# Copies, relus and banks of the last group moved between VectorE and ScalarE, and two orders in the second step, in a fused four-layer graph network

## The chip, the cores and the metric

The kernel runs on one core of a Trainium2 chip. The time is the device time of one execution in microseconds (us); lower is better. It is stated as the median of several executions. The profile is of one further execution.

## The reference, cut to what matters

The input is 128 graphs of 64 nodes with 512 features, float32, and one 64x64 adjacency matrix for each graph. Four layers follow each other, and each is a residual with a layer norm behind it: `x = layernorm(x + layer(x, adj))`.

```python
# layer 0: two hypergraph convolutions, widths 512 -> 1024 -> 512
h = layer_norm(relu(hypergraph_conv(x, adj, W1, b1)), gamma, beta)
y = hypergraph_conv(h, adj, W2, b2) + x
# layer 1: attention by scores of the nodes
s = (x @ w) @ a
A = s[..., :, None] + s[..., None, :]
A = jnp.tanh(A / 8.0) * 8.0
A = jnp.where(A >= 0, A, 0.1 * A)          # the leaky step
A = jnp.exp(A) * A_shape                   # then rows normed, scaled; A @ x @ w
# layer 2: three graph convolutions
x = relu(adj @ (x @ W1) + b1); x = relu(adj @ (x @ W2) + b2); out = adj @ (x @ W3) + b3
# layer 3: attention with 8 heads of 64
out = (0.33 * softmax(q k^T / 8) + 0.33 * adj + 0.33 * exp(-dist)) @ v   # by head
out = out @ W_out + b_out
```

## The kernel before, in words

**Groups.** The 128 graphs are 64 pairs (two graphs fill 128 partitions), and four pairs make a group, so there are 16 groups, numbered 0 to 15. A group's data is one tile of 128 x 4 x 512. `first_half` (for group 0, `first_group`) runs layers 0 and 1 of a group, and `second_half` runs layers 2 and 3. For the last group, number 15, the end of layer 3 is written out on its own in `last_rows`.

**Steps.** Work of three groups is interleaved by a list of names for each step (`start`, `step_1`, `order`, `step_last`, `rest_last`): layers 0 and 1 of group q, layer 2 and the scores of group q-1, and the attention and output of group q-2. The second step, `step_1`, holds layers 0 and 1 of group 1 beside layer 2 of group 0. In most steps a scheduler then orders each engine's instructions by readiness; `behind(key)` forbids it to place an instruction ahead of another one that was noted in `last_add`. `in_turn(engine)` keeps an instruction behind the newest one of that engine. In the start, and for TensorE (PE) and VectorE (DVE) in the last step, everything is in written order.

**Products.** `multiply` makes a 512x512 by 512x512 product with seven block products in place of eight (`B11, T1, T2, B21, T3, B22, T4`, in this order). Each is `product`: 8 recorded matmuls of 128x256, 1.73 us in the trace. `Left.sums` prepares the left side by four VectorE operations `s1` to `s4`: `B11` needs none of them, `T1` needs `s1`, `T2` needs `s2`. In the result, `u1`, `u5`, `u2` are copies of partial sums out of PSUM (the matmul's memory), and four additions or copies write the four quadrants. The block products `B11`, `T2`, `T3` and `T4` add up in one PSUM bank, tile `a`: so `T4` can't start before the addition that reads the bank after `T3` (line 589) is done. The names in the profile are those of the tiles: `a_l2c`, `b_l2c`, `c_l2c` are the banks of layer 2's third product, and so on.

**Small matmuls.** `graph_T` multiplies by the adjacency and turns the result; it fills two PSUM tiles for each half of a group (`duo`), one for each graph of the pairs, which are then copied out. With `both=True` ScalarE (ACT) copies the first of the two and VectorE the second (line 490).

**The end.** `last_rows` turns the last group's softmax (`turn_probs`), multiplies by v (`attend`, tiles `pv`), scales by 0.33 while it copies out (`taken`), and then computes the output pair by pair with `rows_of` (tiles `pp`): addition, statistics (`bn_stats`, `bn_aggr`), square root on ScalarE, reciprocal, scaling, and a store by SyncE (SP). The last pair's two column halves share one PSUM bank, and each half is added and measured on its own.

The queue of a DMA is that of the engine that issues it; all loads and stores in the stretches around the change are on SP. GpSimd (POOL) writes derived weights to DRAM.

Of the kernel before, what the change touches and what calls it, by code (L numbers as in the profile page):

```python
# [8 lines left out]
FP = mybir.dt.float32  # L9
# [5 lines left out]
P = 128  # L15
# [26 lines left out]
def kernel(  # L42
# [427 lines left out]
    def graph_T(src, mat, dst, duo, key, both=False):  # L470

        ps = [ps_gt.tile([P, 4, 2, C], FP, name=f"gt_{key}_{duo}_{g}", tag="gt") for g in range(2)]
        for c in range(4):
            for p in range(2):
                for f in range(2):
                    for g in range(2):
                        rows, c0 = slice(g * C, (g + 1) * C), c * P + f * C  # L480
                        ten.matmul(  # L481
                            ps[g][f * C : (f + 1) * C, c, p, :],
                            src(2 * duo + p)[rows, c0 : c0 + C],
                            mat[rows, 2 * duo + p, :],
                            start=True, stop=True,
                        )
        o = dst[:, :, duo * Q : (duo + 1) * Q].rearrange("p c (a g i) -> p c a g i", a=2, g=2)
        for g in range(2):
            if both and g == 1:
                vec.tensor_copy(o[:, :, :, g, :], ps[g])  # L490
            else:
                act.copy(o[:, :, :, g, :], ps[g])  # L492
# [8 lines left out]
    def behind(key):  # L501
        return tc.issue_after(last_add[key]) if key in last_add else nullcontext()
# [117 lines left out]
    def turned(t):  # L620

        return lambda m, n: t[:, 2 * n : 2 * n + 2, m * Q : (m + 1) * Q]
# [126 lines left out]
    def first_half(g):  # L749
# [83 lines left out]
        yield "w2"  # L833
        with behind(f"l2c_{q - 1}.u2"):
            act.activation(t, t, AF.Tanh, scale=0.125)
        vec.scalar_tensor_tensor(t, t, 0.1, t, ALU.mult, ALU.max)
# [13 lines left out]
        left = Left(f"l1_{q}")  # L850
        for duo in range(2):
            with behind("agg_0.p") if q == 1 else nullcontext():
                graph_T(pair, t, left.t, duo, f"l1_{q}", both=True)
        yield "c3"
        with behind(f"wo_{q - 2}"):
            left.sums()
# [39 lines left out]

    def rows_of(p, ts, quads, u0=0, u1=None, ps=None, ns=range(2)):

        if ps is None:
            ps = ps_acc.tile([P, 2, Q], FP, name=f"pp_{p}", tag="acc")  # L900
        us = range(len(ts))[u0:u1]
        for n in ns:
            for u in us:
                for c in range(KD):
                    ten.matmul(
                        ps[:, n, :], ts[u][:, c, p * P : (p + 1) * P], quads[u][c // 2, n][:, c % 2],
                        start=(n == 0 and u == 0 and c == 0), stop=(u == len(ts) - 1 and c == KD - 1),
                        skip_group_check=True,
                    )
        return ps  # L910
# [162 lines left out]
    def second_half(g):  # L1073
# [18 lines left out]
                    turned(h1.t)(m, n)[:, c], src[:, c], AF.Relu, bias=gb1_col[:, 2 * n + c : 2 * n + c + 1]  # L1092
                )

        for _ in multiply([left], (w_g[0], q), turned(h1.t), f"l2a_{q}", flipped=True, then=relu if q == 0 else None):
            yield "l2a1"
        if q > 0:
            for c in range(KD):
                act.activation(h1.t[:, c, :], h1.t[:, c, :], AF.Relu, bias=gb1_col[:, c : c + 1])
        h1.sums()  # L1100
# [5 lines left out]
        adt = grp.tile([P, G, C], FP, name=f"adt_{q}", tag="adt", bufs=1)  # L1106
        act.activation(adt, g["atc"], AF.Exp, scale=-1.0)
        g["adt"] = adt
        if alone:
            shifted(g, f"l2b_{q}")  # L1110
        yield "gb3"

# [2 lines left out]
        for c2 in range(2):  # L1115
            ps = [ps_gt.tile([P, 2, G, C], FP, name=f"gth2_{q}_{c2}_{h}", tag="gt") for h in range(2)]
            for c in range(2):
                for p in range(G):
                    for f in range(2):
                        for h in range(2):  # L1120
                            rows, c0 = slice(h * C, (h + 1) * C), (2 * c2 + c) * P + f * C
                            ten.matmul(  # L1122
                                ps[h][f * C : (f + 1) * C, c, p, :],
                                g2[rows, p, c0 : c0 + C], g["atc"][rows, p, :], start=True, stop=True,
                            )
            for c in range(2):
                k = 2 * c2 + c
                o = h2.t[:, k, :].rearrange("p (d h t) -> p d h t", d=2, h=2)
                for h in range(2):
                    act.activation(  # L1130
                        o[:, :, h, :], ps[h][:, c].rearrange("p (d a) i -> p d (a i)", d=2),
                        AF.Relu, bias=gb2_col[:, k : k + 1],
                    )
        if not alone:
            shifted(g, f"l0w2_{q + 1}.u2")
        h2.sums()
        yield "gh"
        g3 = big.tile([P, G, D], FP, name=f"g3_{q}", tag="big")
        gen = multiply([h2], (w_g[2], q), nat(g3), f"l2c_{q}", stops=(3, 6),
# [29 lines left out]
        for duo in range(2):  # L1169
            ps = [ps_gt.tile([P, KD, 2, C], FP, name=f"xtp_{q}_{duo}_{h}", tag="gt") for h in range(2)]  # L1170
            for c in range(KD):
                for p in range(2):
                    for h in range(2):
                        rows = slice(h * C, (h + 1) * C)
                        with behind("l1w_1.p6") if q == 0 else nullcontext():
                            ten.transpose(
                                ps[h][:, c, p, :], xg[rows, 2 * duo + p, c * P : (c + 1) * P], identc[rows]
                            )
            o = left.t[:, :, duo * Q : (duo + 1) * Q].rearrange("p c (a g i) -> p c a g i", a=2, g=2)
            for h in range(2):  # L1180
                act.copy(o[:, :, :, h, :], ps[h])  # L1181
        left.sums()
        yield "xT"
        qT = big.tile([P, KD, T], FP, name=f"qT_{q}", tag="big")
# [48 lines left out]
    def last_rows(g, probs, v, left):  # L1233

        q, xg = g["q"], g["x"]
        o = out[q * T : (q + 1) * T, :].rearrange("(p t) d -> t p d", t=P)
        gen = multiply([left], (w_v, q), nat(v), f"v_{q}", stops=(3, 6))
        next(gen)
        yield "v1"
        steps = [[softmax_steps(g, duo, probs[duo], h2) for h2 in range(2)] for duo in range(2)]  # L1240
        for n in range(2):
            for h2 in range(2):
                next(steps[0][h2])
        for n in range(2):
            next(steps[1][0])
        for h2 in range(2):
            next(steps[0][h2])
        next(gen)
        yield "v2"
        left = Left(f"oT_{q}")  # L1250
        pts = turn_probs(g, 0, probs[0])
        whole(gen)
        yield "v"
        taken(0, attend(g, 0, pts, v), left)
        for n in range(2):
            next(steps[1][1])
# [7 lines left out]
        def added(p, ps, n=None):  # L1264
            cols = slice(0, D) if n is None else slice(n * Q, (n + 1) * Q)
            row = xg[:, p, cols]
            vec.tensor_add(row, ps.rearrange("p n f -> p (n f)")[:, cols], row)

        def written(p):
            layer_norm(xg, f"l3_{q}_{p}", (p,))  # L1270
            nc.sync.dma_start(out=o[:, p], in_=xg[:, p])

        ps = projected(0)
# [23 lines left out]
        nc.sync.dma_start(out=o[:, 3], in_=xg[:, 3])  # L1297
        yield "o"

    def softmax_steps(g, duo, ds, h2):  # L1300
# [90 lines left out]
                        )  # L1391
        return ps

    def taken(duo, ps, left):
        o4 = left.t[:, :, duo * Q : (duo + 1) * Q].rearrange("p c (a g i) -> p c a g i", a=2, g=2)
        for gg in range(2):
            act.mul(o4[:, :, :, gg, :], ps[gg], LA)  # L1397

# [177 lines left out]
```

## Time and profile before

| | |
|---|---|
| time, median of 3 runs | 2743.45 us (2742.39 to 2743.74) |
| profiled execution, its own time | 2741.53 us |
| its span, first to last instruction | 2739.8 us |
| TensorE busy | 2720.2 us (99%) |
| VectorE busy | 2079.1 us (76%) |
| ScalarE busy | 804.2 us (29%) |
| DMA | 405.14 MB, mean 148 GB/s |

The profiled execution takes 1.7 us more than its span, and 1.9 us less than the median of the runs. In the views below, the first number of a row of the timeline is its start in us from the start of the span, the second how long it lasted; what stands in brackets is for how long the engine was idle before it, and which instruction of which engine ended that. A row with a count (x8) stands for several instructions merged. A matmul's record overlaps the next one's: they start 0.216 us apart and each lasts 0.379 us.

### The profile page before, as it was taken

To read this page: it belongs to the slowest core of one execution; us is meant where nothing else is said; L and a number is where in the kernel's file an instruction comes from. 1 tells how busy PE (TensorE), PEld (TensorE's weight loads), DVE (VectorE), ACT (ScalarE), POOL (GpSimd) and SP (SyncE) were. 2 spreads that over 40 slices of the span, in tenths; PEclk is the share of its full clock that TensorE was granted. 3 is DMA by queue.
4 is the path that set the end of the run, shared out by engine and by line. 5 is a ranking of instruction groups with operands and counts; after the bars stand their busy time and mean duration, and the time that the engine had idled before them with its cause. 6 is when DMAs were issued, how large, how long until landed. Compare 5 with 4: busy or idle time off the path is not lost.

```text
span 2739.8 us, 67717 instructions
## 1 busy us (share of the span) xinstructions
PE 2720.2 (99%) x28770; PEld 2348.2 (86%) x28770; DVE 2079.1 (76%) x4119; ACT 804.2 (29%) x1442; POOL 38.0 (1%) x71
## 2 busy tenths in 40 slices
PE   9999999999999999999999999999999999999998
PEld 8878888888888888888888888888888888888887
DVE  6877687876877778787786877778777687776866
ACT  3323323232232332322223232232323323232232
POOL 2000000000000000000000000000000000000000
PEclk9999999999999999999999999999999999999999
DMA  8534454454544545445454454545545455454541
GB/s 263 180 120 153 121 174 141 141 166 131 171 132 139 166 129 169 132 143 169 132 166 130 144 164 131 166 126 153 159 131 171 130 161 146 132 164 131 151 126 60
DMA packets 309388, 405.14 MB, mean 148 GB/s; under 512 B 57408, under 2 KB 185184, under 8 KB 309088
## 3 DMA queue, kind: packets, MB, share of 16 engines
q1 hardware_dynamic: 304256, 385.58, 47.4%
q0 software_dynamic: 4832, 15.24, 1.5%
q8 instruction: 228, 3.74, 0.6%
q14 instruction: 72, 0.59, 0.1%
HBM read 369.78 MB, written 30.93 MB: 146 GB/s over the span
## 4 chain that ended last, share of the span: by engine, by line
PE 95%; DVE 3%; ACT 1%; issue 0%; DMA 0%; POOL 0%; DVEq 0%; POOLq 0%
PE a_l0w L539 15%; PE b_l0w L539 7%; PE a_l2b L539 4%; PE a_q L539 4%; PE a_k L539 4%; PE a_l2a L539 4%; PE a_v L539 4%; PE c_l0w L539 4%; PE a_l1w L539 4%; PE a_wo L539 4%; PE a_l2c L539 4%; PE gt_l L481 3%; PE gt_l0h L481 2%; PE b_l1w L539 2%; PE b_l2a L539 2%; PE b_l2b L539 2%
## 5 line engine op out<-in xcount | busy, mean ns | idle before, releaser
L539 PE MATMUL a_l0w<-w2w,aT_l0h 128*128 128x256 f32 x720 | 164.3, 381 | 0.0
L457 DVE BATCH_NORM_STATS2 st_l<-x 128x6 f32<-128x512 f32 x244 | 157.7, 673 | 0.6
L539 PEld LDWEIGHTS a_l0w<-w2w,aT_l0h 128*128 128x128 f32 x720 | 135.6, 190 | 18.8
L463 DVE TENSOR_SCALAR x<-x,mv_l,rs_l 128x512 f32<-128x512 f32 x244 | 119.3, 542 | 2.2
L539 PE MATMUL b_l0w<-w2w,s_l0h 128*128 128x256 f32 x480 | 108.5, 379 | 0.0
L779 ACT ACTIVATE h<-h 128x1024 f32<-128x1024 f32 (+1 forms) x58 | 54.9, 947 | 178.5 <-DVE h L598 157.5
L539 PEld LDWEIGHTS b_l0w<-w2w,s_l0h 128*128 128x128 f32 x480 | 91.1, 190 | 12.5
L1130 ACT ACTIVATE aT_h<-gth,gb_col 128x256 f32<-128x256 f32 x128 | 48.5, 492 | 159.0 <-PE gth L1122 159.0
L447 ACT ACTIVATE rs_l<-mv_l,eps_t 128x4 f32<-128x4 f32 (+1 forms) x64 | 19.0, 297 | 257.0 <-DVE mv_l L458 245.3
L555 DVE TENSOR_TENSOR u_l0w<-a_l0w,b_bc 128x512 f32<-128x512 f32 x56 | 38.6, 690 | 69.2 <-PE a_l0w L539 69.2
L492 ACT COPY aT_l<-gt_l 128x512 f32<-128x512 f32 x146 | 77.1, 596 | 45.7 <-PE gt_l L481 45.7
L539 PE MATMUL a_l1w<-ww,aT_l 128*128 128x256 f32 x360 | 85.7, 381 | 2.1 <-issue 2.1
L539 PE MATMUL a_l2b<-gwbw,aT_h 128*128 128x256 f32 x360 | 86.6, 383 | 0.7 <-ACT aT_oT L1397 0.7
L539 PE MATMUL a_l2c<-gwcw,aT_h 128*128 128x256 f32 x360 | 86.3, 382 | 0.0
L539 PE MATMUL a_q<-aT_xT,wqw 128*128 128x256 f32 x360 | 85.1, 379 | 0.7 <-ACT aT_xT L1181 0.7
L539 PE MATMUL a_l2a<-aT_l,gwaw 128*128 128x256 f32 x360 | 85.0, 379 | 0.0
L539 PE MATMUL a_k<-aT_xT,wkw 128*128 128x256 f32 x360 | 85.0, 379 | 0.0
L539 PE MATMUL a_l0w<-w1aw,aT_l 128*128 128x256 f32 x336 | 80.8, 383 | 0.0
L539 PE MATMUL a_v<-wvw,aT_xT 128*128 128x256 f32 x336 | 80.8, 383 | 0.0
L539 PE MATMUL a_wo<-wow,aT_oT 128*128 128x256 f32 x336 | 79.5, 379 | 0.0
L539 PE MATMUL a_l0w<-w1bw,aT_l 128*128 128x256 f32 x336 | 79.4, 379 | 0.0
L539 PEld LDWEIGHTS a_l1w<-ww,aT_l 128*128 128x128 f32 x360 | 68.5, 190 | 11.6 <-issue 2.3
(528 smaller groups left out, 6488.4 us busy)
## 6 DMA issues: line engine op xcount, KB each, us to landing
w2w<-w2k SPq DMA_DIRECT2D x210, 256.0 KB, 2.6
x<-in_x_dram SPq DMA_DIRECT2D x15, 1024.0 KB, 5.7
w1aw<-w1ak SPq DMA_DIRECT2D x60, 256.0 KB, 2.6
w1bw<-w1bk SPq DMA_DIRECT2D x60, 256.0 KB, 2.7
ww<-wk SPq DMA_DIRECT2D x60, 256.0 KB, 2.8
gwaw<-gwak SPq DMA_DIRECT2D x60, 256.0 KB, 3.1
gwbw<-gwbk SPq DMA_DIRECT2D x60, 256.0 KB, 2.7
gwcw<-gwck SPq DMA_DIRECT2D x60, 256.0 KB, 2.7
```

The lines of the kernel that those rows point to most:

```text
L447: act.activation(rs[:, at], mv[:, at, 1], AF.Sqrt, bias=eps_t)
L457: vec.bn_stats(st, xg[:, p, :])
L463: vec.tensor_scalar(xg[:, p, :], xg[:, p, :], mv[:, p, 0:1], rs[:, p : p + 1], ALU.subtract, ALU.mult)
L481: ten.matmul(ps[g][f * C : (f + 1) * C, c, p, :], src(2 * duo + p)[rows, c0 : c0 + C], mat[rows, 2 * duo + p, :], start=True, stop=True,)
L492: act.copy(o[:, :, :, g, :], ps[g])
L539: ten.matmul(acc[:, blk, :], lhsT, rhs, start=(first and blk == 0 and i == 0), stop=(last and i == n_k - 1), skip_group_check=True,)
L555: last_add[f"{key}.{what}"] = (act.copy(t, ps) if res is None else vec.tensor_add(t, ps, res(m, n))).ins
L779: act.activation(hn, hn, AF.Relu)
L1130: act.activation(o[:, :, h, :], ps[h][:, c].rearrange("p (d a) i -> p d (a i)", d=2), AF.Relu, bias=gb2_col[:, k : k + 1],)
```

## The change

For the last group (15):

- Layer 2's first product applies its relu quadrant by quadrant, as group 0 does, straight behind each addition; the fourth quadrant's relu reads PSUM in place of a copy.
- The relus behind the second product's `gth2` tiles are split: h = 0 on ScalarE, h = 1 on VectorE, as an addition and a maximum. The bias additions and mask work of `shifted` move from ahead of the sums of `h2` to behind them.
- The copies of `xtp` are split in the same way, and so are those of attention's first half (`taken(0, ...)`), whose ScalarE part is now placed ahead of the last exponential.
- In the output of the last pair, each column half has a PSUM bank of its own, so pair 3's matmuls don't wait for an addition. The statistics of pair 2 are interleaved with those of pair 3. The last scaling is made in two halves of 256 columns, each with a store of its own, one issued by SP and one by ScalarE.

In the second step (group 1 beside group 0):

- Both copies of each `gt_l1_1` duo are on ScalarE (`both=q > 1`).
- The leaky operation stands behind the addition after `T3` of `l2c_0` (`l2c_0.d`).

```diff
-        vec.scalar_tensor_tensor(t, t, 0.1, t, ALU.mult, ALU.max)
+        with behind("l2c_0.d") if q == 1 else nullcontext():
+            vec.scalar_tensor_tensor(t, t, 0.1, t, ALU.mult, ALU.max)
...
-                graph_T(pair, t, left.t, duo, f"l1_{q}", both=True)
+                graph_T(pair, t, left.t, duo, f"l1_{q}", both=q > 1)
...
-        if ps is None:
+        fresh = ps is None
+        if fresh:
...
-                        start=(n == 0 and u == 0 and c == 0), stop=(u == len(ts) - 1 and c == KD - 1),
+                        start=(fresh and n == ns[0] and u == 0 and c == 0), stop=(u == len(ts) - 1 and c == KD - 1),
...
-        for _ in multiply([left], (w_g[0], q), turned(h1.t), f"l2a_{q}", flipped=True, then=relu if q == 0 else None):
+        for _ in multiply([left], (w_g[0], q), turned(h1.t), f"l2a_{q}", flipped=True, then=relu if alone else None):
             yield "l2a1"
-        if q > 0:
+        if not alone:
...
-        if alone:
+        if q == 0:
             shifted(g, f"l2b_{q}")
...
-                    act.activation(
-                        o[:, :, h, :], ps[h][:, c].rearrange("p (d a) i -> p d (a i)", d=2),
-                        AF.Relu, bias=gb2_col[:, k : k + 1],
-                    )
+                    cols = ps[h][:, c].rearrange("p (d a) i -> p d (a i)", d=2)
+                    if q == NGRP - 1 and h == 1:
+                        vec.tensor_scalar(o[:, :, h, :], cols, gb2_col[:, k : k + 1], 0.0, ALU.add, ALU.max)
+                    else:
+                        act.activation(o[:, :, h, :], cols, AF.Relu, bias=gb2_col[:, k : k + 1])
...
         h2.sums()
+        if q == NGRP - 1:
+            last_add["h2s"] = newest(DVE)
+            shifted(g, "h2s")
...
-                act.copy(o[:, :, :, h, :], ps[h])
+                if q == NGRP - 1 and h == 1:
+                    vec.tensor_copy(o[:, :, :, h, :], ps[h])
+                else:
+                    act.copy(o[:, :, :, h, :], ps[h])
...
-        taken(0, attend(g, 0, pts, v), left)
-        for n in range(2):
+        next(steps[1][1])
+        with in_turn(ACT):
+            taken(0, attend(g, 0, pts, v), left, both=True)
+        with in_turn(ACT):
             next(steps[1][1])
...
-        written(2)
-
-        st = small.tile([P, 2, 6], FP, name="st_last", tag="st_last", bufs=1)
-        ps = None
+        ps = [projected(3, n=n) for n in range(2)]
+        mv = small.tile([P, 2, 2], FP, name="mv_last", tag="mv_last", bufs=1)
+        s2 = small.tile([P, 6], FP, name="st_last2", tag="st", bufs=4)
+        vec.bn_stats(s2, xg[:, 2])
+        vec.bn_aggr(mv[:, 0, :], s2)
+        rs = small.tile([P, 2], FP, name="rs_last", tag="rs_last", bufs=1)
+        act.activation(rs[:, 0:1], mv[:, 0:1, 1], AF.Sqrt, bias=eps_t)
+        half(0, ps[0])
+        vec.reciprocal(rs[:, 0:1], rs[:, 0:1])
+        vec.tensor_scalar(xg[:, 2], xg[:, 2], mv[:, 0, 0:1], rs[:, 0:1], ALU.subtract, ALU.mult)
+        nc.sync.dma_start(out=o[:, 2], in_=xg[:, 2])
+        half(1, ps[1])
+        vec.bn_aggr(mv[:, 1, :], st.rearrange("p n s -> p (n s)"))
+        act.activation(rs[:, 1:2], mv[:, 1:2, 1], AF.Sqrt, bias=eps_t)
+        vec.reciprocal(rs[:, 1:2], rs[:, 1:2])
         for n in range(2):
-            ps = projected(3, ps, n=n)
-            added(3, ps, n)
-            vec.bn_stats(st[:, n], xg[:, 3, n * Q : (n + 1) * Q])
-        mv = small.tile([P, 1, 2], FP, name="mv_last", tag="mv_last", bufs=1)
-        vec.bn_aggr(mv[:, 0, :], st.rearrange("p n s -> p (n s)"))
-        rs = rstd(mv, 1, "last")
-        vec.tensor_scalar(xg[:, 3], xg[:, 3], mv[:, 0, 0:1], rs[:, 0:1], ALU.subtract, ALU.mult)
-        nc.sync.dma_start(out=o[:, 3], in_=xg[:, 3])
+            cols = slice(n * Q, (n + 1) * Q)
+            vec.tensor_scalar(
+                xg[:, 3, cols], xg[:, 3, cols], mv[:, 1, 0:1], rs[:, 1:2], ALU.subtract, ALU.mult
+            )
+            (nc.sync, nc.scalar)[n].dma_start(out=o[:, 3, cols], in_=xg[:, 3, cols])
...
-            act.mul(o4[:, :, :, gg, :], ps[gg], LA)
+            if both and gg == 1:
+                vec.tensor_scalar_mul(o4[:, :, :, gg, :], ps[gg], LA)
+            else:
+                act.mul(o4[:, :, :, gg, :], ps[gg], LA)
```

`half(n, ps)`, which is new, adds one column half of pair 3 (`xg[:, 3, n * Q : (n + 1) * Q]`) to its bank and measures it: `vec.tensor_add(row, ps[:, n], row)` and `vec.bn_stats(st[:, n], row)`. After the build, the orders of PE and POOL are the same in both kernels; those of VectorE, ScalarE and SP differ only in the places named above.

More of the change, by code (lines that the diff above doesn't have):

```diff
@@ L1262, in projected, with added @@
             return rows_of(p, [left.t], stream.here[w_o, q], ps=ps, ns=range(2) if n is None else (n,))
[L1264 to L1267, printed above, removed]
+        def added(p, ps):
+            row = xg[:, p]
+            vec.tensor_add(row, ps.rearrange("p n f -> p (n f)"), row)
         def written(p):
@@ L1271, in written, with half @@
             nc.sync.dma_start(out=o[:, p], in_=xg[:, p])
+        st = small.tile([P, 2, 6], FP, name="st_last", tag="st_last", bufs=1)
+        def half(n, ps):
+            row = xg[:, 3, n * Q : (n + 1) * Q]
+            vec.tensor_add(row, ps[:, n], row)
+            vec.bn_stats(st[:, n], row)
         ps = projected(0)
@@ L1392, in attend, with taken @@
         return ps
[L1394 removed]
+    def taken(duo, ps, left, both=False):
         o4 = left.t[:, :, duo * Q : (duo + 1) * Q].rearrange("p c (a g i) -> p c a g i", a=2, g=2)
         for gg in range(2):
[L1397 removed]
+            if both and gg == 1:
+                vec.tensor_scalar_mul(o4[:, :, :, gg, :], ps[gg], LA)
+            else:
+                act.mul(o4[:, :, :, gg, :], ps[gg], LA)
     start = """
```

## The prediction

> **What bounds the kernel now.** I read four views: the page, the waits of PE alone, the timeline around each wait, and the granted clock in stretches of 1 us. The page first:
>
> ```profile
> PE 2720.2 (99%) x28770; PEld 2348.2 (86%) x28770; DVE 2079.1 (76%) x4119; ACT 804.2 (29%) x1442; POOL 38.0 (1%) x71
> ```
>
> PE is idle for 2739.8 - 2720.2 = 19.6 us in all, and from 200 to 2600 us for none. No other engine can be worth anything except where it makes PE wait, or behind PE's last matmul. The waits of PE (us in total, times, longest) say where:
>
> ```profile
> PE sps L127 <- DVE hb L127: 4.8, 1, 4.8
> PE a_l1w L539 <- issue: 2.1, 1, 2.1
> PE pp L127 <- DVE x L127: 1.4, 1, 1.4
> PE pp L127 <- ACT aT_oT L1397: 1.3, 1, 1.3
> PE b_l2c L539 <- issue: 1.0, 1, 1.0
> PE a_l2c L539 <- DVE g L589: 1.0, 1, 1.0
> PE a_l2b L539 <- ACT aT_oT L1397: 0.7, 1, 0.7
> PE a_q L539 <- ACT aT_xT L1181: 0.7, 1, 0.7
> ```
>
> The first is the start, which the change leaves alone. The other seven, 8.2 us, are the places that it touches; then comes the tail behind the last matmul. The second step:
>
> ```profile
> 190.09 0.43 DVE L836 SCALAR_TENSOR_TENSOR t<-t 128x256 f32<-128x256 f32 x1 [0.48 <-ACT t L835]
> 190.43 0.68 DVE L589 TENSOR_TENSOR g<-a_l2c,u_l2c 128x512 f32<-128x512 f32 x1
> 191.17 1.99 PE L539 MATMUL a_l2c<-gwct,aT_h 128*128 128x256 f32 x8 [0.98 <-DVE g L589]
> ...
> 196.87 1.88 DVE L1162 TENSOR_TENSOR x<-agg,x 128x512 f32<-128x512 f32 x3
> 198.66 1.28 DVE L490 COPY aT_l<-gt_l 128x512 f32<-128x512 f32 x2
> 199.45 2.52 PE L539 MATMUL a_l1w<-ww,aT_l 128*128 128x256 f32 x8 [2.15 <-issue]
> 201.06 0.69 DVE L518 TENSOR_TENSOR s_l<-aT_l 128x512 f32<-128x512 f32 x1
> 201.85 3.09 PE L539 MATMUL b_l1w<-ww,s_l 128*128 128x256 f32 x8
> ```
>
> VectorE waits 0.48 us for a tanh with the leaky operation at the head of its queue, while the addition that PE needs stands behind it. Later the first product of `l1w` waits until 199.45, just behind the first VectorE copy (198.66 + 0.68), which stands behind four additions. The eight matmuls of `a_l1w` and `b_l1w` last 2.52 and 3.09 us here, where 1.99 is usual. The clock says why (length of the stretch, busy time of PE, PEld, DVE, ACT, POOL, then PEclk):
>
> ```profile
> 200.00:201.00 1.00, 1.00 (x6) 0.84 (x5) 1.00 (x2) 0.00 (x0) 0.16 (x1) 0.86 0.95 316
> 203.00:204.00 1.00, 1.00 (x4) 0.81 (x3) 1.00 (x3) 0.00 (x0) 0.00 (x0) 0.50 0.97 367
> ```
>
> It is halved from about 200.7 to 204.1, for 3.4 us. The end:
>
> ```profile
> 2732.56 1.99 PE L127 MATMUL pp<-wob,aT_oT 128*128 128x256 f32 x8 [1.44 <-DVE x L127]
> 2734.59 0.42 DVE L127 TENSOR_TENSOR x<-pp,x 128x256 f32<-128x256 f32 x1 [1.62 <-PE pp L127]
> 2736.29 0.55 DVE L127 TENSOR_SCALAR x<-x,mv_last,rs_last 128x512 f32<-128x512 f32 x1
> 2736.86 0.33 SPq L1297 DMA_DIRECT2D out_dram<-x  x1
> ```
>
> The last pair's second half starts 1.44 us late, because it shares its bank with the first half, whose addition queues behind pair 2's norm. The store is issued at 2736.86 and 2.9 us later all is over.
>
> **Part 1, the leaky operation.** The addition L589 can start when `t` is formed (L832 from 189.18, next start about 189.52), and end at 190.2 in place of 191.11; `T4` starts at 190.26, not 191.17. PE gains 0.9 there but gives some back: `gt_l` needs `t`, and `t` hangs on VectorE. Leaky itself starts at 190.12 (before 190.09), the exponential behind it ends at 191.0 as before, the addition L598 fills that wait, and everything from the multiplication L840 on is 0.57 earlier. So `gt_l` starts at 194.63, not 195.20: gain **0.57**, with PE idle for 0.5 ahead of it. Bounds 0.48 (the idle time seen) and 0.9.
>
> **Part 2, the copies on ScalarE.** VectorE loses two copies, two steps of 0.60 in its queue; ScalarE gains two of 0.59. ScalarE has nothing else to do there (idle 4.1 us ahead of its next snapshot at 202.06), so nothing waits behind them. Duo 0's copies run at 195.85 and 196.33 and end at 196.92; `a_l1w` starts at 196.97, only 0.2 behind `gt_l`, in place of 199.45. But `T1` needs `s1`, which stays behind the additions and two weight operations on VectorE: 201.06 - 0.57 - 1.20 = 199.29, ready at 199.98. `T1` starts at 200.05, not 201.85, and PE stands idle for 1.35 first. So of 2.1 us the copies themselves give **1.2**; the next late thing is `s1`.
>
> [...] The rows differ: a copy of 128x512 out of PSUM takes 0.69 on VectorE (L490) and 0.59 on ScalarE (L492, mean 596 ns). [...]
>
> **Part 3, the clock.** `T1` took from 201.85 to 204.78, 2.93, where a product takes 1.73: the halved clock cost **1.2**. In the 3.4 us before the drop PE was busy for some 1.3, 37%. [...] The trace shows the drop, so I count 1.2. After the change a like window holds `a_l1w`, part of `T1` and 1.4 us idle: about 58% busy. The last pair's wait of 1.44 left a similar share, and the clock there stayed at 1.00. [...]
>
> From `T2` on, everything is then 0.57 + 1.2 + 1.2 = **2.97** earlier. VectorE gains only 1.8, but has 2.09 idle before L568 at 208.50, which covers the rest. PE does not wait again until 2600, so all of it stays.
>
> **Part 4, the relus of h1.** ScalarE's four relus of 128x512 and a copy end at 2629.47, and only then `aT_oT` frees a bank for `a_l2b`. With relus by quadrants only two of 128x256 (0.48 each) remain behind `T4`'s end at 2627.27: done at 2628.2. The first bank is free at 2629.0, before PE has finished `pv` at 2629.3. The whole wait goes: **0.7**. `s1` is ready at 2628.9, before `T1` needs it.
>
> **Part 5, the relus of h2.** Eight on ScalarE take 2644.02 to 2647.05 (L1130), then `s1` 0.69, then `b_l2c` at 2647.87. Split, the last four start at about 2645.0. VectorE's relu of 128x256 from PSUM is not in the trace: between 0.29 (L730, from SBUF) and 0.43 (an addition of 128x256 from PSUM); I take 0.43, the same memory. Then all end at 2645.8, `s1` at 2646.5, before `B11` is through at 2646.67. Gain 1.04, and 0.16 by which matmul records overlap: **1.2**; 0.8 if a relu takes 0.69. The bias additions and masks, 4.4 us, had covered VectorE's idle time ahead of the relus; they now fall after the sums, from 2648.3 to 2652.7, where 3.7 us were idle before L568. L568 may slip by 0.5, and `T4` needs only the next addition, 3 us later: nothing.
>
> **Part 6, xtp and pv.** The VectorE copy of `xtp` queues behind L610 (2673.12), so it ends at 2674.40 where ScalarE's second ended at 2674.58: **0.19**, not 0.7. For `pv`, ScalarE's exponential stood ahead of the two copies; now one copy on each engine starts at 2715.36 and VectorE's, 0.69 like L490, ends at 2716.05, so `pp` starts at 2716.09, not 2716.63: **0.54**. VectorE waits 1.1 us for `pv` at the head of its queue; its last softmax multiplication moves from 2718.06 to 2719.76. The transposes of that half now start near 2720.0: just covered; if not, 0.1 goes.
>
> **Part 7, the end.** Pair 3's second half follows the first and ends at 2732.85. Pair 2's norm still fits before it (scaling over at 2732.7). Then addition 0.42, statistics 0.43, 0.21, root 0.29, reciprocal 0.16 with the gaps of before: scaling starts at 2734.59. Two halves of about 0.31 in place of 0.55: the later store is issued at 2735.17, not 2736.86: **1.69**. That store has the ScalarE queue, on which this kernel has issued none. ScalarE's own work is over then, and I take SP's times (issue 0.33, landing 2.0); from below -0.1, as it is half the size, from above +0.7, as a load of 128 KB took 2.4 and POOL issues in 0.54.
>
> **Sum.** 2.97 + 0.7 + 1.2 + 0.19 + 0.54 + 1.69 = 7.3 us. The profiled execution, 2741.53, would become 2734.2. The median of the runs is 1.92 above it. Two of the three runs lie 1.1 to 1.35 above the lowest, which is about the clock's price, so I take the median for a run with the drop: 2743.45 - 7.3 = 2736.2.
>
> **The rivals.** A measurement of this kernel can tell about 0.2%, 5.5 us, from no change.
> - *The forecast*, 0.62: gain 6.2 to 8.2, 2735.3 to 2737.3.
> - *The clock gives nothing*, 0.18: the median before is a run without the drop, gain 6.1; or one also drops after, at the 1.35 us ahead of `T1`, 7.3 - 1.2 - 0.2. Time 2737.3 to 2738.6, on either side of 5.5. For it: the share of 58% is near nothing that the trace has tested; against: the like window at the end.
> - *The waits come back on VectorE*, 0.15: `s1` of `h2`, the `pv` copy and the softmax behind it each fall late, and the last store lands 0.7 later: gain 3 to 5, 2738.5 to 2740.5. For it: three parts rest on durations that the trace lacks.
> - *The last store on the new queue*, 0.05: all ends with it, so every us that it takes longer is lost whole. It becomes slower than before when issue and landing take 2.3 + 7.3 = 9.6 us, and by 0.2% at 15. For it: loads have taken up to 11.8 us to land (`wr`); against: those were in a crowded start, and the queues are empty here. Time 2744 to 2750.
>
> Faster by over 0.2%: 0.62, 0.09 of the second, 0.02 of the third: 0.73. Slower by over 0.2%: 0.03. Within: 0.24. The range 2734.8 to 2739.6 leaves out the upper half of the third case, all of the fourth, and some of the first.
>
> **What would show it.** `a_l1w` starting near 197.0, `b_l1w` near 200.05 for 1.9, PEclk 1.00 at 200 to 204; PE's waits on `b_l2c`, `a_l2b` and on `DVE x` gone, `pp` at 0.77, `a_q` near 0.5; the last store issued 1.7 sooner behind PE's last matmul. Wrong would be: a halved clock near 200, or 3 us or more from the last issue to the end.

## The result, and the profile after

| | before | after |
|---|---|---|
| time, median of 14 runs each | 2743.21 us (2741.63 to 2744.45) | 2736.62 us (2736.01 to 2738.87) |
| profiled execution, its own time | 2741.53 us | 2736.76 us |
| its span | 2739.8 us | 2735.0 us |

The ratio is 0.9978, with a 95% interval of 0.9969 to 0.9986: a gain of 6.59 us between the medians, where 7.3 was predicted. In us the interval is 3.8 to 8.5, so the medians alone can't tell 7.3 from the 6.1 of the first rival. The time itself, 2736.62, is close to the predicted 2736.2. The two profiled executions differ by 4.8 us only, and the reason for that is told below.

The page's line of busy times shows 15.9 us of idle PE time (2735.0 less 2719.1), 3.7 fewer than before:

```profile
PE 2719.1 (99%) x28770; PEld 2348.1 (86%) x28770; DVE 2081.7 (76%) x4125; ACT 802.8 (29%) x1440; POOL 37.9 (1%) x71
```

The waits of PE, in the same columns as before (us in total, times, longest):

```profile
PE sps L127 <- DVE hb L127: 5.3, 1, 5.3
PE b_l1w L539 <- issue: 1.1, 1, 1.1
PE gt_l L481 <- DVE t L849: 0.9, 2, 0.6
PE pp L127 <- ACT aT_oT L1426: 0.9, 1, 0.9
PE a_q L539 <- ACT aT_xT L1190: 0.5, 1, 0.5
...
PE gt_l L481 <- issue: 0.4, 1, 0.4
PE a_l1w L539 <- ACT aT_l L492: 0.2, 1, 0.2
```

Gone are the waits on `a_l2c`, `b_l2c`, `a_l2b` and the one of `pp` for `DVE x`. Those on `a_q` and `pp` are smaller. The wait of 2.1 on `a_l1w` has become one of 1.1 on `b_l1w`: that is the foretold wait for `s1`. Two entries don't belong to the change. The first wait is 0.5 us longer than before, in the start, and the 0.4 on "issue" inside `gt_l` stands where the first trace had nothing.

The second step in the timeline of after (start, duration, and in brackets the idle time before and what ended it):

```profile
190.29 0.68 DVE L589 TENSOR_TENSOR g<-a_l2c,u_l2c 128x512 f32<-128x512 f32 x1
...
190.90 0.41 DVE L837 SCALAR_TENSOR_TENSOR t<-t 128x256 f32<-128x256 f32 x1
...
195.52 2.10 PE L481 MATMUL gt_l<-t,x 64*64 64x64 f32 x128 [0.62 <-DVE t L849]
...
196.74 2.05 ACT L492 COPY aT_l<-gt_l 128x512 f32<-128x512 f32 x4 [3.09 <-PE gt_l L481]
...
197.86 1.99 PE L539 MATMUL a_l1w<-ww,aT_l 128*128 128x256 f32 x8 [0.24 <-ACT aT_l L492]
198.98 0.68 DVE L267 TENSOR_TENSOR wqt<-wqb,wqb 128x512 f32<-128x512 f32 x1
199.58 0.68 DVE L268 TENSOR_TENSOR wqt<-wqb,wqt 128x512 f32<-128x512 f32 x1
...
200.19 0.68 DVE L518 TENSOR_TENSOR s_l<-aT_l 128x512 f32<-128x512 f32 x1
...
200.97 1.97 PE L539 MATMUL b_l1w<-ww,s_l 128*128 128x256 f32 x8 [1.11 <-issue]
...
202.77 1.89 PE L539 MATMUL a_l1w<-ww,s_l 128*128 128x256 f32 x8
```

The addition L589 now stands ahead of the leaky operation (L837). All four copies are on ScalarE, and `a_l1w` follows 0.24 behind `gt_l`. `T1` (`b_l1w`) lasts 1.97, not 3.09, and `T2` starts at 202.77 where it started at 204.78. By then this execution was already 0.77 us late from the start of the program, so the gain on this stretch is 2.01 + 0.77 = 2.78.

The end, with the last scaling in two halves and a store behind each. The second fence is the trace's list of DMA issues in the last stretch (queue and count, KB each, us from issue to landing):

```profile
2731.12 0.73 DVE L127 TENSOR_SCALAR x<-x,mv_last,rs_last 128x256 f32<-128x256 f32 x2
2731.57 0.33 SPq L1323 DMA_DIRECT2D out_dram<-x  x1
2731.89 0.39 ACTq L1323 DMA_DIRECT2D out_dram<-x  x1
```

```profile
out_dram<-x SPq DMA_DIRECT2D x2, 256.0 KB, 2.0
out_dram<-x SPq DMA_DIRECT2D x1, 128.0 KB, 1.7
out_dram<-x ACTq DMA_DIRECT2D x1, 128.0 KB, 1.8
```

The later store is issued 0.77 behind the start of the scaling, and the span ends 3.1 behind that (2735.0 less 2731.89). Before it was 0.57, for one scaling of 512 columns, and 2.9 (2739.8 less 2736.86). With the spans to two digits, 2734.99 and 2739.76, it is 3.10 and 2.90.

**Part by part.** I compared the start of every PE tile in the two traces and took the steps in their difference; the start's 0.77 and two stops inside `gt_l` (below) are apart.

| step | predicted | in the two traces |
|---|---|---|
| 1 leaky, at `gt_l` | 0.57 | 0.45 |
| 2 copies, at `b_l1w` | 1.2 | 1.2 |
| 3 clock, at `T2` | 1.2 | 1.13 |
| 4 relus of `h1`, at `a_l2b` | 0.7 | 0.73 |
| 5 relus of `h2`, at `b_l2c` | 1.2 | 1.12 |
| 6 `xtp` at `a_q`, `pv` at `pp` | 0.19 + 0.54 | 0.14 + 0.46 |
| 7 the end, behind `pp` | 1.69 | 1.35 |
| sum | 7.3 | 6.6 |

The profiled pair shows 4.8 in place of 6.6, because the execution of after started 0.77 late and lost another 1.02 at two places that the change doesn't touch: PE stood still inside the small matmuls of `gt_l` near 585 us and near 1259 us, and all behind them is 0.71 and 0.31 later. The 0.4 on "issue" among the waits is what the trace shows of it as idle time.

### The profile page after: what moved, and what is told of

It is laid out like the page before. It is cut to its first block, busy times and chain, and to the rows that moved or that the text cites. A ratio compares the mean times of both kernels' runs of the same rounds, so it can differ in the third digit from the quotient of the medians.

```text
span 2735.0 us, 67727 instructions
## 1 busy us (share of the span) xinstructions
PE 2719.1 (99%) x28770; PEld 2348.1 (86%) x28770; DVE 2081.7 (76%) x4125; ACT 802.8 (29%) x1440; POOL 37.9 (1%) x71
## 4 chain that ended last, share of the span: by engine, by line
PE 96%; DVE 3%; ACT 1%; issue 0%; DMA 0%; DVEq 0%; SPq 0%
PE a_l0w L539 15%; PE b_l0w L539 7%; PE a_l2b L539 4%; PE a_q L539 4%; PE a_k L539 4%; PE a_l2a L539 4%; PE a_v L539 4%; PE c_l0w L539 4%; PE a_l1w L539 4%; PE a_wo L539 4%; PE a_l2c L539 4%; PE gt_l L481 3%; PE gt_l0h L481 2%; PE b_l2a L539 2%; PE b_l1w L539 2%; PE b_q L539 2%
## 5 line engine op out<-in xcount | busy, mean ns | idle before, releaser
L539 PEld LDWEIGHTS a_l2c<-gwcw,aT_h 128*128 128x128 f32 x360 | 67.2, 190 | 11.6 <-ACT u_l2c L555 3.0
```

The costliest lines, as they stand in the source:

```text
L539: ten.matmul(acc[:, blk, :], lhsT, rhs, start=(first and blk == 0 and i == 0), stop=(last and i == n_k - 1), skip_group_check=True,)
```

## The experiments

Each kernel is the changed one with the edit shown; one is the kernel before itself, without an edit, and the last has its edits on top of the one ahead of it. A time behind "before" is that of the kernel before on the same chip in the same session.

**The end alone** (`e1_tail_only`): the second step's two edits undone.

```diff
-        with behind("l2c_0.d") if q == 1 else nullcontext():
-            vec.scalar_tensor_tensor(t, t, 0.1, t, ALU.mult, ALU.max)
+        vec.scalar_tensor_tensor(t, t, 0.1, t, ALU.mult, ALU.max)
...
-                graph_T(pair, t, left.t, duo, f"l1_{q}", both=q > 1)
+                graph_T(pair, t, left.t, duo, f"l1_{q}", both=True)
```

> The changed kernel with both edits of the second step undone: the leaky operation is free again, and VectorE makes the second copy of each duo of group 1. My theory, that the parts are independent and add up: what is left is the last group's share, which in the two profiles is 0.73 (relus of h1) + 1.12 (relus of h2) + 0.14 (xtp) + 0.46 (pv) + 1.38 (from the last matmuls to the end) = 3.8 us, so 2739.4 where the kernel before has 2743.2, ratio 0.9986. Rival, that VectorE hands the second step's waits on to the end or that the parts overlap: a gain under 2.5 or over 5 us. In the trace a_l1w waits for 2.1 us again and T1 of l1w lasts either 2.9 us (the clock is halved) or 1.9.

Measured: 2738.91 (21 runs) against 2742.78 (49 runs), 3.87 less, ratio 0.9987 (0.9981 to 0.9994, so 1.6 to 5.2 us). That agrees with what the traces said of the last group, 0.73 + 1.12 + 0.60 + 1.35 = 3.80, and in this kernel's own trace the steps come back at the same places: 1.13 at `b_l2c`, 0.14 at `a_q`, 0.46 at `pp`. The second step of this kernel holds a surprise. It is that of the kernel before, with the same gap of 2.15 us, and yet nothing in it runs slowly:

```profile
200.76 1.97 PE L539 MATMUL a_l1w<-ww,aT_l 128*128 128x256 f32 x8 [2.15 <-issue]
203.16 1.97 PE L539 MATMUL b_l1w<-ww,s_l 128*128 128x256 f32 x8 [0.43 <-PE a_l1w L539]
204.96 1.89 PE L539 MATMUL a_l1w<-ww,s_l 128*128 128x256 f32 x8
```

From `a_l1w` to `T2` it is 4.20 us here and 5.33 in the trace of before: the halved clock costs 1.13, but not in every execution.

**The second step alone** (`e2_step2_only`): everything in the last group undone, back to the lines of the kernel before; the two edits of the second step stay.

> The kernel before with the two edits of the second step alone. My theory: 2.8 us faster than before where the clock was halved before (0.45 by the leaky operation's place, 1.2 by the copies, 1.1 to 1.2 by the clock), ratio 0.9990; the clock stays at 1.00 around 200 us. Rival, the clock gives nothing in the usual run: 1.6 us, ratio 0.9994. The end of the trace is that of before: b_l2c waits 1.0, pp 1.3 and 1.4, the store 2.1 us behind the last matmul.

Measured: 2740.64 (13 runs) against 2742.78, 2.14 less, ratio 0.9991 (0.9983 to 0.9999, so 0.3 to 4.7 us). This lies between the 2.8 of a kernel before that always loses the clock and the 1.6 of one that never does, but the interval is too wide to tell the two apart. The trace does better: against the first trace of before it gives 0.46 for the leaky operation, 1.20 for the copies and 1.11 for the clock. With the run above the two halves give 6.0 of the 6.6.

**The copies back on both engines** (`e3_copies_back`):

```diff
-                graph_T(pair, t, left.t, duo, f"l1_{q}", both=q > 1)
+                graph_T(pair, t, left.t, duo, f"l1_{q}", both=True)
```

> The changed kernel with only the copies of group 1 back on both engines; the leaky operation stays behind the addition. My theory: T4 of l2c_0 still starts with the addition before it done, 0.4 us behind the product ahead of it and not 1.36, and a_l1w waits for over 2 us again, because the VectorE copy stands behind four additions; b_l1w then starts about 1.2 us later than in the changed kernel, and the clock is halved in it if a wait of 2.1 us is what halves it: 1.2 to 2.4 us slower than the changed kernel, 2737.8 to 2739.0. Rival, that the leaky operation alone removed the wait chain: within 0.5 us of the changed kernel.

Measured: 2738.24 (21 runs) against 2742.78, ratio 0.9983 (0.9977 to 0.999): 4.54 less, so about 2.0 of the gain hang on the copies (1.6 by the medians of the two kernels themselves). In its trace `T1` and `T2` start 1.35 later than in after (0.16 of it from the start), with the wait of 2.1 back ahead of `a_l1w` and the clock at full. So 1.2 is the price of the copies alone, as the prediction had it. What the medians show beyond that, 0.4 to 0.8, would fit executions in which the clock falls, but it isn't shown: the medians of the kernel before itself went from 2742.25 to 2743.21 between sessions, and only 5 of the 21 runs here list a mean clock under 1.000. This kernel and the one with the end alone differ by the leaky operation's place only. Between their traces `a_l1w` starts 0.84 apart (200.76 and 199.92), of which 0.38 is there from the start: the other 0.46 is part 1 by itself.

**The kernel before, once more** (`e10_before_again`): no edit.

> The kernel before, once more, for a second trace of it. If the drop of the clock near 200 us belongs to the program, it is there again: b_l1w takes 3.1 and PEclk is about 0.5 at 201 to 204. [...] Stray stops of PE inside gt_l, 0 in the first trace and up to 1.6 in others, come back in some size.

Measured: one execution, 2743.33, span 2741.6. The clock falls again, now at 200.29 and again for 3.41 us. But PE also stood still inside `gt_l` in two places, where the first trace had nothing:

```profile
PE gt_l L481 <- issue: 1.2, 2, 0.9
```

The two traces of one program differ by 1.8 us in span: 0.1 of it is there at `T2`, and the rest comes behind two of the `gt_l` of later groups (1.14 by 1262 us, 0.56 more by 2441). So these stops are in the kernel before too, and one profiled pair can't decide a difference of 1 to 2 us.

**When the clock fell.** In the trace of before the granted clock is at 0.50 from 200.72 to 204.13, for 3.41 us, and full on both sides. It is halved for as long in the other two traces that show it near 200 us: from 200.29 in the second trace of before, and from 200.77 in the kernel with four copies on VectorE, below. Here are the 3.41 us ahead of the halved stretch and the stretch itself in before (length, then busy time of PE, PEld, DVE, ACT, POOL, then PEclk), and the 3.41 us ahead of it in its second trace:

```profile
197.31:200.72 3.41, 1.27 (x6) 1.17 (x7) 3.41 (x7) 0.59 (x1) 0.48 (x1) 1.00 0.87 266
200.72:204.13 3.41, 3.41 (x10) 2.28 (x9) 3.38 (x6) 0.59 (x1) 1.08 (x2) 0.50 0.98 316
```

```profile
196.88:200.29 3.41, 1.26 (x47) 1.10 (x39) 3.41 (x7) 0.91 (x2) 0.54 (x1) 1.00 0.80 235
```

The clock is halved once more at the end of both traces of the pair. In before that begins at 2736.82, 2.3 us behind PE's last matmul (2732.56 + 1.99), with PE busy for 1.15 in the 3.41 us ahead of it; in after it begins at 2734.59, 5.2 behind the last one (2725.78 + 3.62), with PE idle all that time:

```profile
2733.41:2736.82 3.41, 1.15 (x6) 0.67 (x4) 1.76 (x5) 0.29 (x1) 0.00 (x0) 1.00 0.10 35
2736.82:2739.80 2.98, 0.00 (x0) 0.00 (x0) 0.01 (x1) 0.00 (x0) 0.00 (x0) 0.50 0.23 88
```

```profile
2731.18:2734.59 3.41, 0.00 (x0) 0.00 (x0) 0.68 (x2) 0.00 (x0) 0.00 (x0) 1.00 0.23 77
2734.59:2735.00 0.41, 0.00 (x0) 0.00 (x0) 0.00 (x0) 0.00 (x0) 0.00 (x0) 0.50 0.00 0
```

The kernel with the end alone and the one with the copies back have the same gap of 2.15 us ahead of `a_l1w`, and their clock stays full behind it, first the former, then the latter:

```profile
199.00:200.00 1.00, 0.00 (x0) 0.00 (x0) 1.00 (x3) 0.25 (x1) 0.10 (x1) 1.00 1.02 362
200.00:201.00 1.00, 0.24 (x1) 0.27 (x2) 1.00 (x3) 0.00 (x0) 0.00 (x0) 1.00 0.80 226
201.00:202.00 1.00, 1.00 (x6) 0.87 (x6) 1.00 (x3) 0.00 (x0) 0.00 (x0) 1.00 0.76 222
```

```profile
199.00:200.00 1.00, 0.08 (x1) 0.11 (x1) 1.00 (x3) 0.00 (x0) 0.00 (x0) 1.00 0.94 271
200.00:201.00 1.00, 1.00 (x5) 0.90 (x6) 1.00 (x3) 0.00 (x0) 0.00 (x0) 1.00 1.01 368
```

In both, any 3.41 us that hold the whole gap have PE busy for at most 1.26 (3.41 less 2.15), as in the two traces of before (1.27 and 1.26). So neither the gap nor PE's busy time around it tells the traces with a halved clock from those with a full one, and what else decides it is not shown.

In the second step of after the clock is full throughout (1.00 from 190 to 204 us), and PE is busy for at least 2.05 of any 3.41 us there (0.60), counted in steps of 0.1 us; this is the emptiest place:

```profile
197.56:200.97 3.41, 2.05 (x12) 1.47 (x9) 3.38 (x7) 1.81 (x4) 1.49 (x3) 1.00 0.86 266
```

That the missing gap is why the clock stays full here is my estimate; two kernels kept it with the gap.

How often the clock fell can be bounded from the runs. Each run lists its mean granted clock to three digits, and 3.41 us at half speed take 0.0006 from it (3.41 x 0.5 / 2740), so by this estimate a run that lists 1.000 had no such stretch. Of the 49 runs of the kernel before beside the first experiments, 23 list 1.000, with a median of 2742.27, and 26 list 0.999, with a median of 2743.09. Of the 23 beside the later ones 9 list 1.000 and 14 list 0.999; there the medians of the two sorts don't keep that order (2742.97 and 2742.20 in one session, 2741.97 and 2742.43 in the other). In some of those at 0.999 only the fall in the last microseconds may have counted: 5 of the 14 runs of after list 0.999 too. So the kernel before paid the 1.1 us in at most 40 of 72 runs, and the price itself can be read from the traces only.

**All four copies on VectorE** (`e9_copies_vector`), to make the gap longer:

```diff
-            if both and g == 1:
+            if key == "l1_1" or both and g == 1:
```

> All four gt_l1_1 copies on VectorE. This makes the gap ahead of a_l1w longer than before's 2.1 us by one copy: about 2.7 us. [...]

Measured: one execution, 2741.38. PE waits 2.7 us ahead of `a_l1w`, is busy for 0.94 of the 3.41 us up to 200.77 (0.28), and the clock is halved from 200.77 to 204.18:

```profile
PE a_l1w L539 <- DVE aT_l L490: 2.7, 1, 2.7
PE gt_l L481 <- issue: 2.4, 3, 1.2
```

```profile
197.36:200.77 3.41, 0.94 (x4) 0.87 (x5) 3.41 (x7) 0.00 (x0) 0.26 (x1) 1.00 0.81 277
```

```profile
199.83 2.89 PE L539 MATMUL a_l1w<-ww,aT_l 128*128 128x256 f32 x8 [2.70 <-DVE aT_l L490]
202.87 2.61 PE L539 MATMUL b_l1w<-ww,s_l 128*128 128x256 f32 x8
205.32 1.89 PE L539 MATMUL a_l1w<-ww,s_l 128*128 128x256 f32 x8
```

The clock fell, as I had expected, and its price was smaller than I had counted on: `T2` starts 3.0 later than in after (2.54, and 0.48 that this execution was ahead), not 3.5 to 4.5. With four copies ahead of it, `s1` starts only at 202.09 and ends at 202.77 (202.09 + 0.68), and PE would have waited for it after `a_l1w` at a full clock too (199.83 + 1.97 = 201.80). Only `T1`, 2.45 to the next start in place of 1.8, paid. Here the halved clock in `a_l1w` cost nothing, because the next thing was late anyway.

**One store at the end** (`e4_one_store`):

```diff
-        for n in range(2):
-            cols = slice(n * Q, (n + 1) * Q)
-            vec.tensor_scalar(
-                xg[:, 3, cols], xg[:, 3, cols], mv[:, 1, 0:1], rs[:, 1:2], ALU.subtract, ALU.mult
-            )
-            (nc.sync, nc.scalar)[n].dma_start(out=o[:, 3, cols], in_=xg[:, 3, cols])
+        vec.tensor_scalar(xg[:, 3], xg[:, 3], mv[:, 1, 0:1], rs[:, 1:2], ALU.subtract, ALU.mult)
+        nc.sync.dma_start(out=o[:, 3], in_=xg[:, 3])
```

> The changed kernel with one scaling of 512 columns and one store by SP for the last pair, in place of two of each. My theory: the two scalings of 256 came out at 0.73 us together where one of 512 takes 0.55, and the stores landed after 1.7 and 1.8 us where one of 256 KB takes 2.0, so the split gains nothing: the end of the span, counted from the last matmul, is within 0.2 us of the changed kernel. Rival, that two queues help the store: this one is 0.3 us or more later.

Measured: one execution, 2737.22, span 2735.5 (2735.45). It had more stops inside `gt_l` than after, and its last scaling starts 0.84 later (2731.96 against 2731.12); but its span is only 0.46 longer. So from the last scaling to the end it takes 0.38 less. One scaling of 0.55 brings its store out 0.58 behind its start, where the second of the halves' stores needs 0.77; and from the issue to the end it is 2.91 (2735.45 less 2732.54) against 3.10, though the whole store takes 2.0 to land and the halves 1.7 and 1.8. What fills the time behind the landing, no view shows. The split of the last store costs about 0.4, more than the 0.2 that I had allowed.

**The masks ahead of the relus** (`e5_masks_ahead`): the relus of `h2` stay split, but the bias and mask work goes back ahead of the sums.

```diff
-        if q == 0:
+        if alone:
             shifted(g, f"l2b_{q}")
...
         h2.sums()
-        if q == NGRP - 1:
-            last_add["h2s"] = newest(DVE)
-            shifted(g, "h2s")
```

> The changed kernel with the bias additions and masks of the last group back where they were, ahead of the relus of h2 on VectorE; the relus stay split over both engines. My theory: the move is what makes the split worth anything. VectorE is busy with 4.4 us of additions and masks from about the end of the second product until 2.6 us behind the start of gth2, so its four relus start about 1.1 us later than ScalarE's, s1 is ready about as late as when ScalarE made all eight, and b_l2c starts 2.5 to 3.1 us behind the start of a_l2c (changed kernel 1.92, before 3.04). Rival, that the split alone does it: 2.1 or less.

Measured: one execution, 2736.85. First after, then this kernel:

```profile
2642.36 1.79 DVE L1134 TENSOR_SCALAR aT_h<-gth,gb_col 128x256 f32<-128x256 f32 x4 [2.69 <-PE gth L1124]
2643.13 1.99 PE L539 MATMUL a_l2c<-gwcw,aT_h 128*128 128x256 f32 x8
...
2644.26 0.69 DVE L518 TENSOR_TENSOR s_h<-aT_h 128x512 f32<-128x512 f32 x1
...
2645.05 1.97 PE L539 MATMUL b_l2c<-gwcw,s_h 128*128 128x256 f32 x8
```

```profile
2642.20 2.02 PE L539 MATMUL a_l2c<-gwcw,aT_h 128*128 128x256 f32 x8
...
2643.00 1.26 DVE L1134 TENSOR_SCALAR aT_h<-gth,gb_col 128x256 f32<-128x256 f32 x3
...
2645.15 1.97 PE L539 MATMUL b_l2c<-gwcw,s_h 128*128 128x256 f32 x8 [0.93 <-PE a_l2c L539]
```

In after VectorE stands idle for 2.7 us and takes up the relus the moment that `gth` is there. With the masks ahead it is still busy with them, the last three relus start at 2643.00, and `b_l2c` starts 2.95 behind `a_l2c` in place of 1.92. Before it was 3.04. So of part 5's 1.12 nearly all is lost again: the split of the relus is worth next to nothing without an idle VectorE to take its half.

**The `pv` copies on ScalarE alone** (`e6_pv_scalar`), with the exponential still behind them:

```diff
-            taken(0, attend(g, 0, pts, v), left, both=True)
+            taken(0, attend(g, 0, pts, v), left)
```

> The changed kernel with both copies of attention's first half on ScalarE, still ahead of the last exponential. My theory: most of the 0.45 us came from taking the exponential out of the way, and the split gives the rest: with 0.58 and a step of 0.49 the second copy ends 1.07 behind the first one's start, so pp starts about 2.05 us behind the last pv's start group (1.16 us of pv and 1.1 of copies) against 2.05 in the changed kernel and 2.47 before; counted from the first pv matmul 2.3 us (changed 2.05, before 2.47). Rival, the split alone is what counts: 2.45 or more.

Measured: one execution, 2737.82, with a stop of 1.2 inside a `gt_l`. PE waits 1.2 ahead of `pp` where it waits 0.9 in after, and `pp` starts 0.29 later against the tiles before it. So the split is worth 0.29 of part 6's 0.46, and putting the exponential behind the copies the other 0.17: the larger share is the split's, where I had expected the exponential's.

**The weight work behind `s1`** (`e7_wq_behind`): the trace of after names the next late thing, two VectorE operations (L267, L268) of a derived weight that stand ahead of `s1` in the second step. Here they are issued a place later in the step's list, and behind the last sum of `l1w_1`:

```diff
-        a.c3 sumsq2 a.p1 b.xT sumsk a.p2 b.q1 a.ln1 b.q rows2 b.k1 b.k prep b.dots
+        a.c3 a.p1 sumsq2 b.xT sumsk a.p2 b.q1 a.ln1 b.q rows2 b.k1 b.k prep b.dots
...
-            stream.make_half(w_q)
+            with behind("l1s_1") if who == "sumsq2" else nullcontext():
+                stream.make_half(w_q)
```

> The changed kernel with the last two derived-weight operations of w_q (two of 0.60 us on VectorE) placed behind the sums of l1_1 in the second step, so that s1 is no longer behind them. My theory, that s1 is what T1 of l1w waits for (1.1 us in the trace of the changed kernel): b_l1w starts 1.1 to 1.2 us sooner, straight behind a_l1w, and the whole is 1.1 us faster than the changed kernel, 2735.5. Rival: the xtp transposes or the first products of q then wait for VectorE, and it comes out at 2736.6 or above.

Measured: 2734.80 (8 runs) against 2742.33 (12 runs), ratio 0.9972 (0.9962 to 0.9983). It is 7.53 below before. Against after it is 0.9 better by the differences to their own runs of before, and 1.8 by the two medians; the intervals of the two ratios overlap, so the times don't show it, but the trace does (1.3 ahead of after at `T1`, 0.1 of it from the start). `s1` starts at 198.87, and `T1` follows `a_l1w` without a wait:

```profile
198.87 0.68 DVE L518 TENSOR_TENSOR s_l<-aT_l 128x512 f32<-128x512 f32 x1
...
199.65 1.96 PE L539 MATMUL b_l1w<-ww,s_l 128*128 128x256 f32 x8
```

**The same, with one store and `xtp` ahead of an addition** (`e8_three_more`): the edit of `e4_one_store`, and the last addition of `wo_14`, kept for later and issued behind VectorE's `xtp` copies.

```diff
+        elif key == f"wo_{NGRP - 2}":
+            pending.append(lambda: vec.tensor_add(dst(1, 0), pa, res(1, 0)))
...
+        if q == NGRP - 1:
+            last_add["xtc"] = newest(DVE)
+            with behind("xtc"):
+                pending.pop()()
```

> The kernel with the weight work behind s1 of l1w_1, and two edits more: the last pair is scaled and stored in one piece, by SP, and the last addition of wo_14 (L610 of the changed kernel) stands behind VectorE's xtp copies. My theory: one store ends 0.3 us sooner than two halves, as it did alone; and the copies no longer stand behind an addition of 0.42, so that a_q starts 0.2 to 0.4 sooner: 2734.8 - 0.3 - 0.3 = 2734.2, about 9.0 below the kernel before. The rival: a_q then waits for ScalarE's own second copy or for the bank that the late addition holds, and the second edit gives 0 or costs up to 0.6: 2734.5 to 2735.1.

Measured: 2734.64 (7 runs) against 2742.25 (11 runs), ratio 0.9973 (0.9962 to 0.9984): 7.61 below before, which can't be told from the 7.53 of the kernel without the two edits. In its trace the end comes 0.4 sooner behind the last matmul, as with one store alone. `a_q` starts 0.16 sooner, between my theory's 0.2 to 0.4 and the rival's nothing. VectorE's first copy now starts with ScalarE's, as soon as `xtp` is there, and takes 0.69, so it still ends last (2669.44), and PE starts 0.10 behind it:

```profile
2668.72 1.09 ACT L1193 COPY aT_xT<-xtp 128x512 f32<-128x512 f32 x2 [3.85 <-PE xtp L1185]
2668.75 1.29 DVE L1191 COPY aT_xT<-xtp 128x512 f32<-128x512 f32 x2 [0.34 <-PE xtp L1185]
2669.54 1.97 PE L540 MATMUL a_q<-aT_xT,wqw 128*128 128x256 f32 x8 [0.35 <-ACT aT_xT L1193]
```

Steps of this size are below what the medians can tell.

## Why the prediction came out as it did

**Right.** The mechanisms and their places held: every wait that was said to go is gone, the two that were said to shrink shrank, and the new wait on `b_l1w` stands where it was said to. `a_l1w` follows `gt_l` by 0.24 (said: 0.2), the clock stays full in the second step of after (1.00 from 190 to 204 us), and the relus' gains on `h1` and `h2` are within 0.1. The last two rivals did not come about: no wait of over 0.1 came back on VectorE at `s_h`, at `pp` or ahead of the last softmax, and the store on ScalarE's queue lands in 1.8. Of the signs of being wrong, one came up: it is 3.1 from the last issue to the end, where 3 or more was to be a warning. It cost 0.2 (part 7). Parts 4 and 7 have no kernel of their own; their sizes are read from the traces of after and of the end alone.

**Part 3, counted in full.** The step "The trace shows the drop, so I count 1.2" has nearly the right price: 1.13 in the two traces, and 5.33 less 4.20 between before and the kernel with the end alone. The 1.2 came from setting `T1`'s 2.93 against 1.73, the distance of products without a wait; behind a wait it is 1.80 at full clock (203.16 to 204.96). Its weight in the median is wrong. "I take the median for a run with the drop" does not hold: at least 32 of 72 runs of before had none, so on average the clock gives at most 0.6 of the 1.13. The first rival, that the clock gives nothing, holds for the runs without a drop; its other half, a drop in after as well, did not come in the profiled execution (PEclk 1.00 from 190 to 204 us), and for the runs without a trace it is not shown. The share that part 3 set against a drop (58%; 0.60 in the trace of after) decides nothing by itself: two kernels kept the clock full at 0.37. That the traces' parts add up to 6.6 and the medians differ by 6.59 is therefore partly chance: about half of the clock's price is missing on average, and stops inside `gt_l` and differences in the start, which are in both kernels, are of the same size.

**Part 7, 1.35 and not 1.69.** Everything up to the last scaling went as told. The mis-sized term is "two halves of about 0.31": from the start of the scaling to the issue of the later store it took 0.77, not 0.58. That is 0.19, and the issue came 1.55 sooner behind PE, not 1.69. The rest is the new queue, from whose issue to the end it takes 3.10, where SP's store took 2.90: +0.20, within the bounds of -0.1 and +0.7. The kernel with one store shows both terms at once: 0.38 better.

**Part 1, 0.45 and not 0.57.** The addition and leaky moved as told (leaky 0.04 later, exponential as before). But the two multiplications L840 and L841 (L839 and L840 before) had L598 between them before; now they are neighbours, and the second overwrites what the first reads. It starts 0.45 behind it (191.83 and 192.28), where the next one, L845, which doesn't need its result, follows by 0.34: 0.12 given back. The bounds of 0.48 and 0.9 didn't cover that order.

**Parts 5 and 6.** VectorE's relu of 128x256 out of PSUM takes 0.48 (L1134, median 480 ns), near the 0.43 of the addition that it was sized by, so `s1` was late by a little: 1.12. At `pp` PE waits 0.89 where 0.77 was said: VectorE's copy is the last to end, as told and with the 0.69 told, but it starts 0.04 behind ScalarE's, and PE starts 0.10 behind its end where 0.04 was counted. At `a_q` too the copy ends 0.19 sooner, as told, and PE follows it by 0.10: 0.14. The cover named for part 5 (VectorE idle ahead of the relus once the masks have moved) is what the run with the masks ahead took away, and the gain went with it.

## What to carry to other kernels

When PE waits, ask which instruction stands at the head of the late engine's queue, not which engine is busy: here an idle ScalarE took 1.2 us off VectorE's queue, moving two weight operations a place back gave about as much again in the trace, and a split of eight relus was worth next to nothing until the masks were out of VectorE's way. A price seen once in a trace, such as a clock that falls, needs a count of how often it falls before it is set against a median. Splitting the very last operation and its store into halves put the last issue 0.2 later here, and the end came another 0.2 later behind that issue, though each half landed sooner.

## What the runs showed of the hardware that I had not expected

- The granted clock was halved for 3.41 us near 200 us behind a gap in PE's work of 2.15 us in both traces of before, and behind one of 2.70 in the kernel with four copies on VectorE. Behind a gap of 2.15 in the kernel with the end alone and in the one with the copies back it stayed full. What decides between the two isn't shown.
- In 10 of the 12 traces PE stands still for 0.2 to 1.2 us at a time inside the small matmuls of `gt_l` of some group (near 585, 1259, 1932, 2100 or 2440 us), with no instruction that it waits for; the idle time that the trace shows for it went from 0 to 2.4 us in an execution, in the kernel before as well (0 and 1.2). No run here took it away, and its cause stays open. Stops of this size could account for much of the spread of some 3 us between runs; that isn't shown.
- In the second step of after, VectorE's L598 starts 0.33 us behind the 128x256 operation L837, and L845 0.34 behind L841. It was 0.45 between L840 and L841, where the second overwrites what the first reads, and between L845 and the small L846, where the second reads what the first wrote.
